# Who adds the seven products: VectorE from PSUM, or TensorE onto banks that already hold sums

## The chip, the cores and the metric

One NeuronCore of a Trainium2 chip runs the whole program in one launch. The metric is device time in microseconds (us), the median over runs. The engines have short names in what follows: PE is TensorE (matmuls), PEld its weight loads, DVE is VectorE, ACT is ScalarE, POOL is GpSimd, and SP issues DMAs. All data are fp32.

## The reference, cut to what matters

Two decoder-like layers work on `x` (2 batches x 1024 tokens x 256). Layer 0 is a windowed cross-attention and a grouped linear feed-forward, layer 1 a cross-attention with a sigmoid and then a soft mixture of experts. The change is in the last of these only:

```python
logits = jnp.einsum('bsd,etd->bset', xn, se)          # 1024 tokens x 1024 slots
dispatch = jax.nn.softmax(logits, axis=1)
slots = jnp.einsum('bsd,bset->betd', xn, dispatch)    # per batch: 1024 slots x 256
h = jax.nn.gelu(slots @ w1, approximate=False)        # w1: 256 x 1024   <- the change
processed = h @ w2                                    # w2: 1024 x 256
combine = jax.nn.softmax(logits.reshape(b, s, e * t), axis=-1)
out = jnp.einsum('bnd,bsn->bsd', processed.reshape(b, e * t, d), combine)
```

The product `slots @ w1` of each batch is 1024 x 256 by 256 x 1024.

## The kernel before, in words

**The stage.** `hidden(b)` computes gelu(slots @ w1) of batch `b`, transposed: 1024 hidden units on the partitions, in eight chunks of 128, and 1024 slots along the free dimension, in two halves of 512. It runs twice (b = 0, 1), each time between `gather` (slots from dispatched tokens, line 409, whose last transposes are `pst`, line 450) and `processed` (h @ w2, products `pp`, line 586), which `combined` follows (products `pc`, also line 586).

**Seven products instead of eight.** The 2 x 2 block product is made in the Strassen-Winograd way. `sum_weights` has made the seven left blocks `lefts` from w1, `sum_slots` makes the seven right blocks from the slots on DVE: `t1` (line 498), `t2` (line 500), a difference in place (line 501), `t4` (line 502). Chunks j and j + 4 go together, so there are four groups, j = 0 to 3, and in each the products are, by their index in `lefts` and `rights`:

- p1 (index 0) and p2 (index 1): the slots as they are. p1 and p2 of a group need none of the sums.
- p5 (index 4) uses t1, p6 (index 5) uses t2, p7 (index 6) the difference of line 501, p4 (index 3) uses t4, p3 (index 2) the slots of the other half.

With u = p1 + p6 the four results are h11 = p1 + p2, h12 = u + p5 + p3, h21 = u + p7 + p4 and h22 = u + p7 + p5. Each goes through gelu on ACT into the `mh` tiles, which `processed` reads.

**How a product is made.** In the version before, `alone(i, j)` takes a PSUM bank of its own and issues one 128x128 by 128x512 matmul into it (line 511; the trace shows each as two matmul records). PSUM has eight banks in two pools of four (`ps_0`, `ps_1`), which successive allocations take in turn. p1 is copied to SBUF by ACT (line 545, `begin`); after that DVE makes the additions of the group, each with one operand in SBUF and one in PSUM, result in SBUF (lines 552, 556, 557, 561, 563, 567 and 570): seven of them. Four gelus per group (line 521) read and write SBUF in place.

**What sets the order.** `manual_schedule(engines=IN_ORDER)` keeps PE and DVE in the order in which the code names the instructions; before, it stands around the first three products, `turn_slots` and `sum_slots` only, and the rest of `hidden` is placed by the scheduler. ACT is in program order from the logits on (`ACT_ORDER`, line 1349), so it takes its instructions as written: the last `dispatch(1, 7)` (line 398, the exponential of the last 128 tokens of batch 1, which follows a POOL addition of line 395) comes before the first copy of `hidden(0)`. `turn(1, 0, True)`, four 128x512 transposes on DVE (line 308) and sixteen DMAs, is done inside `hidden(0)`, after group 1.

Of the kernel before, what the change touches and what calls it, by code (L numbers as in the profile page):

```python
# [10 lines left out]
AF = mybir.ActivationFunctionType  # L11
ALU = mybir.AluOpType
# [22 lines left out]
OC = FF // P  # L35
# [7 lines left out]
EC = NSLOT // P  # L43
# [4 lines left out]
IN_ORDER = {mybir.EngineType.DVE, mybir.EngineType.PE}  # L48
# [4 lines left out]
def tile_kernel(  # L53
# [19 lines left out]
    nc = tc.nc  # L73
# [9 lines left out]
    def bank(name, side=0):  # L83
        return ps[side].tile([P, 512], FP, tag="bank", name=name)
# [92 lines left out]
    def in_order(x, dc):  # L177

        return x[:, :, dc].rearrange("p i t n -> p t i n")
# [110 lines left out]
    def turn(q, h, late=False, move=True):  # L290

        if q < QB:
            tr = pools["m12"].tile(
                [P, R4, EC // 2, QT, SQ], FP, tag="tr", name=f"tr_{q}_{h}", bufs=2
            )
        else:

            if h == 0:
                trs[q] = keep[0].tile(
                    [P, 2, R4, EC // 2, QT, SQ], FP, tag=f"ec_{q % QB}", name=f"tr_{q}"
                )
            tr = trs[q][:, h]
        half = ecs[q][:, h]
        for t in range(QT):
            ins = nc.vector.transpose(  # L308
                tr[:, :, :, t, :].rearrange("p r c n -> p c r n"),
                half[:, t, :].rearrange("p (c r n) -> p c r n", c=EC // 2, r=R4),  # L310
            )
            if late:
                tc.keep_in_program_order(ins)
        turned_squares[q, h] = tr
        if move:
            turn_moves(q, h)
# [3 lines left out]
    def turn_moves(q, h):  # L320
        half, tr = ecs[q][:, h], turned_squares[q, h]
        to = half.rearrange("p a b -> p (a b)").rearrange("p (k i n) -> p k i n", i=R4, n=SQ)
        for i in range(R4):
            for r in range(R4):
                nc.sync.dma_start(
                    out=to[ts(r, SQ), :, i, :],
                    in_=tr[ts(i, SQ), r].rearrange("p c t n -> p (c t) n"),
                )
# [115 lines left out]
    def turn_slots(b, c):  # L444

        if c % 2 == 0:
            pts[c // 2] = bank(f"pst_{b}_{c // 2}", 1)
        pt = pts[c // 2]
        for dc in range(DC):
            nc.tensor.transpose(  # L450
                pt[:, ds(dc * 2 * P + (c % 2) * P, P)], sls[c][:, ts(dc, P)], ident
            )
        if c == EC - 3:
            for dc in range(DC):
                slots_out(b, c // 2, dc)

    def slots_out(b, c2, dc):
        nc.vector.tensor_scalar(
            slTs[b][1][:, dc, ts(c2 - 2, 2 * P)], pts[c2][:, ts(dc, 2 * P)],
            gx[:, dc : dc + 1], None, ALU.mult,  # L460
        )
# [18 lines left out]
    def sum_slots(b):  # L480

        x, y = slTs[b]
        b11, b21 = in_order(x, 0), in_order(x, 1)
        b12, b22 = y[:, 0, :], y[:, 1, :]

        def by_square(v):
            return v.rearrange("p (t i n) -> p t i n", t=QT, i=R4)


        t0, t1_ = (  # L490
            keep[b].tile([P, QT, XW], FP, tag=f"xh_{i}", name=f"sl_sums_{b}_{i}").rearrange(
                "p t d -> p (t d)"
            )
            for i in range(2)
        )
        t1, t2, t4 = t0[:, 0:512], t0[:, 512:1024], t1_[:, 0:512]
        slots_out(b, EC // 2 - 1, 0)
        nc.vector.tensor_tensor(by_square(t1), by_square(b12), b11, ALU.subtract)
        slots_out(b, EC // 2 - 1, 1)
        nc.vector.tensor_tensor(t2, b22, t1, ALU.subtract)  # L500
        nc.vector.tensor_tensor(b12, b22, b12, ALU.subtract)
        nc.vector.tensor_tensor(by_square(t4), b21, by_square(t2), ALU.subtract)
        rights[b] = [b11, b21, b22, t4, t1, t2, b12]

    def hidden(b):


        def alone(i, j):
            to = bank(f"pmh_{b}_{j}_{i}", nb[0] % 2)
            nb[0] += 1  # L510
            nc.tensor.matmul(  # L511
                to,
                lhsT=lefts[i][:, ts(j, P)],
                rhs=in_order(slTs[b][0], i) if i < 2 else rights[b][i],
                start=True,
                stop=True,
            )
            return to

        def gelu(h):  # L520
            nc.scalar.activation(h, h, AF.Gelu)  # L521

        NU = OC // 2

        with tc.manual_schedule(engines=IN_ORDER):
            p1s = [alone(0, 0)]
            turn_slots(b, EC - 1)
            p1s.append(alone(0, 1))
            p2 = alone(1, 0)
            sum_slots(b)  # L530
        hs = {}

        def begin(j):

            for g in range(2):
                for u in range(2):
                    fc = j + u * NU
                    if fc % 2 == 0:
                        hss[b, g, fc // 2] = keep[b].tile(
                            [P, 2, 512], FP, tag=f"lg_{4 * g + fc // 2}", name=f"mh_{b}_{g}_{fc}"  # L540
                        )
            hs[j] = [
                hss[b, g, (j + u * NU) // 2][:, j % 2, :] for g in range(2) for u in range(2)
            ]
            nc.scalar.copy(hs[j][0], p1s[j])  # L545

        begin(0)
        for j in range(NU):
            h11, h21, h12, h22 = hs[j]
            p5 = alone(4, j)  # L550
            p6 = alone(5, j)
            ins = nc.vector.tensor_tensor(h12, h11, p6, ALU.add)
            if b == 0 and j == 2:
                tc.keep_in_program_order(ins)
            p7 = alone(6, j)
            nc.vector.tensor_tensor(h21, h12, p7, ALU.add)
            nc.vector.tensor_tensor(h22, h21, p5, ALU.add)  # L557
            gelu(h22)
            if j + 1 < NU:
                begin(j + 1)  # L560
            nc.vector.tensor_tensor(h12, h12, p5, ALU.add)
            p4 = alone(3, j)
            nc.vector.tensor_tensor(h21, h21, p4, ALU.add)
            gelu(h21)
            if j > 0:
                p2 = alone(1, j)
            nc.vector.tensor_tensor(h11, h11, p2, ALU.add)
            gelu(h11)
            p3 = alone(2, j)
            nc.vector.tensor_tensor(h12, h12, p3, ALU.add)  # L570
            gelu(h12)
            if j + 2 < NU:
                p1s.append(alone(0, j + 2))
            if b == 0 and j == 1:
                turn(1, 0, True)

    nb = [0]

# [220 lines left out]
    with (  # L799
# [124 lines left out]
        with tc.tile_pool(name="p0", bufs=1) as p0, tc.tile_pool(name="a0", bufs=2) as a0:  # L924
# [52 lines left out]
            for c in range(C0):  # L977
                for dc in range(DC):
# [4 lines left out]
                        start=(dc == 0),  # L983
# [6 lines left out]
            for c in range(C0):  # L990
                for dc in range(DC):
# [4 lines left out]
                        start=(dc == 0),  # L996
# [10 lines left out]
            for dc in range(DC):  # L1007
                pws = [bank(f"pwk_{dc}_{e}") for e in range(2)]
                for c in range(C0):
                    for e in range(2):  # L1010
# [5 lines left out]
                            start=True,  # L1016
# [9 lines left out]
            for g in range(NBW // 2):  # L1026
                pw = bank(f"pvw_{g}")
                for i in range(2):
                    for c in range(C0):
# [4 lines left out]
                            start=True,  # L1034
# [102 lines left out]
        with (  # L1137
# [36 lines left out]
            for c in range(C1):  # L1174
                for dc in range(DC):
# [4 lines left out]
                        start=(dc == 0),  # L1180
# [14 lines left out]
            for dc in range(DC):  # L1195
# [4 lines left out]
                    start=(dc == 0),  # L1200
# [6 lines left out]
            for b in range(B):  # L1207
                for e in range(2):
                    to = vblk1[e * NK : (e + 1) * NK, b, :, e, :]
# [63 lines left out]
            for c in range(C1):  # L1273
# [4 lines left out]
                    start=True,  # L1278
# [8 lines left out]
            for q in range(NQ):  # L1287
                b = q * QN // S
                oTs[q] = a1.tile([P, C1, QN], FP, tag="oT", name=f"oT_{q}")
                for c in range(C1):  # L1290
# [8 lines left out]
                    for j in range(NPR):  # L1299
# [5 lines left out]
                            start=True,  # L1305
# [26 lines left out]
                    for j in range(NPR):  # L1332
# [4 lines left out]
                            start=True,  # L1337
# [20 lines left out]
    for u in range(1, B * ST + 2):  # L1358
        b, s = divmod(u, ST)
# [31 lines left out]
    for b in range(B):  # L1391
# [25 lines left out]
        if b == 0:  # L1417
            dispatch(1, ST - 1)
        hidden(b)
        with tc.manual_schedule(engines=IN_ORDER):  # L1420
            processed(b)
# [70 lines left out]
```

## Time and profile before

| | |
|---|---|
| device time, median of 3 runs | 423.03 us (422.97 to 423.04) |
| span of the profiled execution, first to last instruction | 421.3 us |
| around the span (median less span) | 1.7 us |
| granted TensorE clock over the span | 0.999 |
| PE busy | 416.1 us (99%) |
| DVE busy | 316.7 us (75%) |
| ACT busy | 131.1 us (31%) |
| products of `hidden` (L511), 56 matmuls, two records each | 592 ns a record, one every 0.43 us |
| additions of `hidden` on DVE, 56 | 0.68 us each, one every 0.60 us |
| gelus of `hidden` on ACT, 32 | 0.63 us each |

The profiled execution has no time of its own outside its span; the sum is made on the span, and the 1.7 us around it are taken as fixed.

How to read it: busy time of PE says only that matmuls overlap one another; whether PE waited is seen from the starts of its records. In a timeline the first column is the start of a run of like instructions in us from the start of the span, the second its length, `xN` how many, and the bracket at the end the idle time of the engine before it and who ended it.

### The profile page before, as it was taken

The numbers are of one execution on the slowest core, as the hardware profiler recorded it, in microseconds if no ns is written. First come the engines' busy times: TensorE is split into PE (matmuls) and PEld (weight loads), VectorE is DVE, ScalarE is ACT, GpSimd is POOL, SyncE is SP. The second block draws the span as 40 slices with busy tenths as digits, with TensorE's granted clock in tenths as the row PEclk, the third lists the DMA queues.
The fourth block names the chain that finished last, engine by engine and source line by source line (L and its number), as shares of the span: only waits on it lengthen the run. The fifth ranks groups of instructions, "written<-read, shape, count | busy, mean of one in ns | idle before, by whom it ended". The sixth has DMA issues, their size and how long they took to land.

```text
span 421.3 us, 6298 instructions
## 1 busy us (share of the span) xinstructions
PE 416.1 (99%) x2270; PEld 310.4 (74%) x2270; DVE 316.7 (75%) x712; ACT 131.1 (31%) x265; POOL 73.8 (18%) x86
## 2 busy tenths in 40 slices
PE   9999999999999999999999999999999999999996
PEld 7888988888444454444488744999998864499996
DVE  2676878745578669978769889977985589776956
ACT  1145568513444522244641554300000004420000
POOL 2112333211101220104948900000000000000000
PEclk9999999999999999999999999999999999999999
DMA  6999993404523332120052664450022566620003
GB/s 255 418 414 426 376 366 122 181 36 123 149 102 103 47 49 31 29 44 2 0 213 102 125 99 73 68 88 2 0 85 48 120 122 97 91 42 2 2 2 100
DMA packets 99425, 50.03 MB, mean 119 GB/s; under 512 B 87873, under 2 KB 94401, under 8 KB 97857
## 3 DMA queue, kind: packets, MB, share of 16 engines
q1 hardware_dynamic: 99394, 49.63, 42.1%
q8 instruction: 18, 0.29, 0.3%
q14 instruction: 13, 0.11, 0.1%
HBM read 32.74 MB, written 6.30 MB: 93 GB/s over the span
## 4 chain that ended last, share of the span: by engine, by line
PE 89%; DVE 7%; issue 1%; POOL 1%; ACT 1%; DVEq 0%; ACTq 0%
PE psl L409 13%; PE pmt L879 13%; PE pc L586 12%; PE pp L586 12%; PE pmh L511 10%; PE pl L256 7%; PE pq L1233 3%; PE po L907 3%; PE pf L1247 3%; PE psg L1301 2%; PE psc L1055 2%; PE poT L1333 2%; PE po L1101 2%; DVE lg L264 1%; PE pvw L1030 1%
## 5 line engine op out<-in xcount | busy, mean ns | idle before, releaser
L879 PE MATMUL pmt<-wg 128*128 128x256 f32 x256 | 58.9, 386 | 0.1
L409 PE MATMUL psl<-xh,lg 128*128 128x258 f32 x256 | 56.8, 380 | 0.0
L256 PE MATMUL pl<-seT,xhT 128*128 128x512 f32 x128 | 56.1, 594 | 0.2 <-DVE rmax L275 0.2
L879 PEld LDWEIGHTS pmt<-wg 128*128 128x128 f32 x256 | 48.9, 193 | 7.8 <-ACT wg L868 0.5
L409 PEld LDWEIGHTS psl<-xh,lg 128*128 128x128 f32 x256 | 48.1, 190 | 7.4 <-issue 0.5
L256 PEld LDWEIGHTS pl<-seT,xhT 128*128 128x128 f32 x128 | 24.1, 190 | 29.2 <-issue 25.7
L395 POOL TENSOR_TENSOR lg<-lg,mb 128x1024 f32<-128x1024 f32 x13 | 33.2, 2591 | 27.2 <-ACT mb L203 25.3
L279 ACT ACTIVATE ec<-lg,nm 128x1024 f32<-128x1024 f32 x16 | 18.4, 1148 | 39.7 <-DVE nm L264 38.0
L586 PEld LDWEIGHTS pp<-ms,mh 128*128 128x128 f32 x256 | 29.4, 192 | 1.3 <-issue 0.7
L586 PE MATMUL pp<-ms,mh 128*128 128x128 f32 x256 | 30.0, 276 | 0.1
L521 ACT ACTIVATE mh<-mh 128x512 f32<-128x512 f32 x32 | 19.2, 628 | 20.8 <-DVE mh L557 19.2
L511 PE MATMUL pmh<-slT,ms 128*128 128x512 f32 x48 | 24.2, 592 | 0.0
L868 ACT ACTIVATE wg<-wg,less 128x255 f32<-128x255 f32 x56 | 23.3, 495 | 0.1
L1310 ACT ACTIVATE sg<-psg 128x512 f32<-128x512 f32 x32 | 16.5, 602 | 18.2 <-PE psg L1301 18.2
L586 PE MATMUL pp<-m_sums,mh 128*128 128x128 f32 x192 | 22.1, 275 | 0.0
L586 PE MATMUL pc<-pr,ec 128*128 128x128 f32 x192 | 22.1, 275 | 0.0
L586 PEld LDWEIGHTS pp<-m_sums,mh 128*128 128x128 f32 x192 | 21.8, 192 | 0.0
L586 PEld LDWEIGHTS pc<-pr,ec 128*128 128x128 f32 x192 | 21.8, 192 | 0.0
L398 ACT ACTIVATE lg<-lg 128x1024 f32<-128x1024 f32 x16 | 16.1, 1045 | 18.2 <-POOL lg L395 18.2
L545 ACT COPY mh<-pmh 128x512 f32<-128x512 f32 x8 | 4.6, 570 | 50.2 <-PE pmh L511 50.2
L308 DVE STREAM_TRANSPOSE tr<-ec 128x512 f32<-128x512 f32 x32 | 19.8, 674 | 0.0
L597 DVE TENSOR_TENSOR mh<-mh,mh 128x1024 f32<-128x1024 f32 x16 | 18.5, 1218 | 0.5 <-PE pp L586 0.5
(193 smaller groups left out, 670.6 us busy)
## 6 DMA issues: line engine op xcount, KB each, us to landing
wg<-in_wff_dram SPq DMA_DIRECT2D x5, 2052.0 KB, 10.2
ec<-tr SPq DMA_DIRECT2D x128, 64.0 KB, 2.3
wg<-in_wff_dram SPq DMA_DIRECT2D x4, 1026.0 KB, 12.7
xT<-in_xT_dram SPq DMA_DIRECT2D x4, 512.0 KB, 13.8
x<-in_x_dram SPq DMA_DIRECT2D x4, 512.0 KB, 15.9
d_a<-tr_a SPq DMA_DIRECT2D x4, 512.0 KB, 2.6
hTa<-d_a SPq DMA_DIRECT2D x16, 128.0 KB, 3.0
xhT<-tr_m SPq DMA_DIRECT2D x64, 32.0 KB, 2.0
```

What stands on the lines that cost most here:

```text
L256: nc.tensor.matmul(pl, lhsT=xhTs[q][:, dc, ts(t, P)], rhs=in_order(seT[:, n], dc), start=(dc == 0), stop=(dc == DC - 1),)
L279: nc.scalar.activation(ecs[q][:, :, t, :], lg.rearrange("p (h n) -> p h n", h=2), AF.Exp, bias=nm[:, 1:2], scale=-1.0, accum_out=zcs[b][:, ...
L308: ins = nc.vector.transpose(tr[:, :, :, t, :].rearrange("p r c n -> p c r n"), half[:, t, :].rearrange("p (c r n) -> p c r n", c=EC // 2, ...
L395: engine.tensor_tensor(lgs[b][s], lgs[b][s], mbs[b], ALU.add)
L409: nc.tensor.matmul(pz[:, 0:XW], lhsT=lgs[b][s][:, ts(c, P)], rhs=xhs[b * QB + s // QT][:, s % QT, :], start=(s == 0), stop=(s == ST - 1),)
L511: nc.tensor.matmul(to, lhsT=lefts[i][:, ts(j, P)], rhs=in_order(slTs[b][0], i) if i < 2 else rights[b][i], start=True, stop=True,)
L521: nc.scalar.activation(h, h, AF.Gelu)
L586: nc.tensor.matmul(to, lhsT=left(k, m), rhs=right[:, k, :], start=(k == 0), stop=(k == QT - 1),)
L597: nc.vector.tensor_tensor(dst, x, y, op)
L868: nc.scalar.activation(w, w, AF.Identity, bias=less[:, oc : oc + 1])
L879: nc.tensor.matmul(pm[:, ts(hc, D)], lhsT=w1g[:, oc, ts(hc, P)], rhs=w2g[:, oc, :], start=(oc == 0 and hc == 0), stop=(oc == OC - 1 and hc ...
L1310: nc.scalar.activation(sg[:, j, :], psgs[j], AF.Tanh, scale=0.5 * DH1**-0.5)
```

## The change

Per group there are now three PSUM banks, a, b and c, in place of seven:

- bank a: p1, copied to SBUF by ACT as before; then p2 is accumulated onto it by PE, and gelu reads the bank (h11).
- bank b: p6, to which DVE adds the copy of p1 in place; later p7 is accumulated onto it by PE, DVE adds p5 to that into SBUF (h22, then gelu in place), and last p4 is accumulated onto it, and gelu reads the bank (h21).
- bank c: p5, copied to SBUF by ACT (a copy that was not there before); DVE writes bank b + that copy into bank c; p3 is accumulated onto it, and gelu reads the bank (h12).

So DVE makes three additions a group, two of which write PSUM, ACT two copies and four gelus, three of which read PSUM, and PE seven matmuls, four of them onto a bank that holds something. All of `hidden` is now in written order on PE and DVE. The written order is also another one: p2 of group 0 comes before p6 and p5 as it did, but p6 now stands before p5, groups 0 and 1 start together, and p7 and p3 of a group come one group later, p4 two groups later. In the built program the first two `pp` matmuls of `hidden(0)`'s successor stand before its last five products.

```diff
-        def alone(i, j):
-            to = bank(f"pmh_{b}_{j}_{i}", nb[0] % 2)
-            nb[0] += 1
+        def onto(key, i, j, first=True):
+            if first:
+                banks[key, j] = bank(f"pmh_{b}_{j}_{key}", nb[0] % 2)
+                nb[0] += 1
+            to = banks[key, j]
             nc.tensor.matmul(
                 to,
                 lhsT=lefts[i][:, ts(j, P)],
                 rhs=in_order(slTs[b][0], i) if i < 2 else rights[b][i],
-                start=True,
+                start=first,
                 stop=True,
+                skip_group_check=not first,
             )
...
-        with tc.manual_schedule(engines=IN_ORDER):
-            p1s = [alone(0, 0)]
-            turn_slots(b, EC - 1)
-            p1s.append(alone(0, 1))
-            p2 = alone(1, 0)
-            sum_slots(b)
...
-        begin(0)
-        for j in range(NU):
-            h11, h21, h12, h22 = hs[j]
-            p5 = alone(4, j)
-            p6 = alone(5, j)
-            ins = nc.vector.tensor_tensor(h12, h11, p6, ALU.add)
...
-            p7 = alone(6, j)
-            nc.vector.tensor_tensor(h21, h12, p7, ALU.add)
-            nc.vector.tensor_tensor(h22, h21, p5, ALU.add)
-            gelu(h22)
-            if j + 1 < NU:
-                begin(j + 1)
-            nc.vector.tensor_tensor(h12, h12, p5, ALU.add)
-            p4 = alone(3, j)
-            nc.vector.tensor_tensor(h21, h21, p4, ALU.add)
-            gelu(h21)
-            if j > 0:
-                p2 = alone(1, j)
-            nc.vector.tensor_tensor(h11, h11, p2, ALU.add)
-            gelu(h11)
-            p3 = alone(2, j)
-            nc.vector.tensor_tensor(h12, h12, p3, ALU.add)
-            gelu(h12)
-            if j + 2 < NU:
-                p1s.append(alone(0, j + 2))
-            if b == 0 and j == 1:
-                turn(1, 0, True)
+        def p1(j):
+            begin(j)
+            nc.scalar.copy(hs[j][0], onto("a", 0, j))
+        def p2(j):
+            onto("a", 1, j, first=False)
+        def gelu_11(j):
+            gelu(hs[j][0], banks["a", j])
+        def p6(j):
+            t = onto("b", 5, j)
+            nc.vector.tensor_tensor(t, t, hs[j][0], ALU.add)
+        def p5(j):
+            t = onto("c", 4, j)
+            nc.scalar.copy(hs[j][3], t)
+            nc.vector.tensor_tensor(t, banks["b", j], hs[j][3], ALU.add)
+        def p7(j):
+            t = onto("b", 6, j, first=False)
+            nc.vector.tensor_tensor(hs[j][3], t, hs[j][3], ALU.add)
+            gelu(hs[j][3], hs[j][3])
+        def p3(j):
+            gelu(hs[j][2], onto("c", 2, j, first=False))
+        def p4(j):
+            gelu(hs[j][1], onto("b", 3, j, first=False))
+        with tc.manual_schedule(engines=IN_ORDER):
+            p1(0)
+            turn_slots(b, EC - 1)
+            p1(1)
+            p2(0)
+            sum_slots(b)
+            p6(0)
+            p5(0)
+            p6(1)
+            p5(1)
+            gelu_11(0)
+            p2(1)
+            gelu_11(1)
+            p7(0)
+            p3(0)
+            for j in range(2, NU):
+                p1(j)
+                p4(j - 2)
+                p6(j)
+                p5(j)
+                if j > 2:
+                    p2(j - 1)
+                    gelu_11(j - 1)
+                p7(j - 1)
+                p3(j - 1)
+                if b == 0 and j == 2:
+                    turn(1, 0)
+            p7(NU - 1)
+            p4(NU - 2)
+            p3(NU - 1)
+            p2(NU - 1)
+            gelu_11(NU - 1)
+            p4(NU - 1)
```

More of the change, by code (lines that the diff above doesn't have):

```diff
@@ L505, in hidden @@
     def hidden(b):
-        def alone(i, j):
-            to = bank(f"pmh_{b}_{j}_{i}", nb[0] % 2)
-            nb[0] += 1
+        NU = OC // 2
+        banks = {}
+        def onto(key, i, j, first=True):
[3 more added lines that the diff above has]
+            to = banks[key, j]
             nc.tensor.matmul(
@@ L514, in alone, with gelu @@
                 rhs=in_order(slTs[b][0], i) if i < 2 else rights[b][i],
-                start=True,
+                start=first,
                 stop=True,
+                skip_group_check=not first,
             )
             return to
-        def gelu(h):
-            nc.scalar.activation(h, h, AF.Gelu)
-        NU = OC // 2
-        with tc.manual_schedule(engines=IN_ORDER):
-            p1s = [alone(0, 0)]
-            turn_slots(b, EC - 1)
-            p1s.append(alone(0, 1))
-            p2 = alone(1, 0)
-            sum_slots(b)
+        def gelu(dst, src):
+            nc.scalar.activation(dst, src, AF.Gelu)
         hs = {}
@@ L544, in begin @@
             ]
-            nc.scalar.copy(hs[j][0], p1s[j])
-        begin(0)
-        for j in range(NU):
-            h11, h21, h12, h22 = hs[j]
-            p5 = alone(4, j)
-            p6 = alone(5, j)
-            ins = nc.vector.tensor_tensor(h12, h11, p6, ALU.add)
-            if b == 0 and j == 2:
-                tc.keep_in_program_order(ins)
-            p7 = alone(6, j)
-            nc.vector.tensor_tensor(h21, h12, p7, ALU.add)
-            nc.vector.tensor_tensor(h22, h21, p5, ALU.add)
-            gelu(h22)
-            if j + 1 < NU:
-                begin(j + 1)
-            nc.vector.tensor_tensor(h12, h12, p5, ALU.add)
-            p4 = alone(3, j)
-            nc.vector.tensor_tensor(h21, h21, p4, ALU.add)
-            gelu(h21)
-            if j > 0:
-                p2 = alone(1, j)
-            nc.vector.tensor_tensor(h11, h11, p2, ALU.add)
-            gelu(h11)
-            p3 = alone(2, j)
-            nc.vector.tensor_tensor(h12, h12, p3, ALU.add)
-            gelu(h12)
-            if j + 2 < NU:
-                p1s.append(alone(0, j + 2))
-            if b == 0 and j == 1:
-                turn(1, 0, True)
+        def p1(j):
+            begin(j)
+            nc.scalar.copy(hs[j][0], onto("a", 0, j))
```

## The prediction

> **What bounds the kernel now.** First the page: busy times, and the engines' shares of the chain that ended last.
>
> ```profile
> PE 416.1 (99%) x2270; PEld 310.4 (74%) x2270; DVE 316.7 (75%) x712; ACT 131.1 (31%) x265; POOL 73.8 (18%) x86
> PE 89%; DVE 7%; issue 1%; POOL 1%; ACT 1%; DVEq 0%; ACTq 0%
> ```
>
> PE carries the chain; DVE has 7% of it. The question is whether that DVE share lies in the changed stage, so next come the windows: the two passes of `hidden`, from p1 of group 0 to the first `pp` (columns: stretch, its length, then busy time of PE, PEld, DVE, ACT and POOL, granted clock, DMA share, GB/s).
>
> ```profile
> 239.20:264.30 25.10, 24.73 (x60) 10.69 (x59) 22.97 (x38) 13.62 (x21) 2.65 (x2) 1.00 0.59 88
> 343.30:367.80 24.50, 24.50 (x61) 10.75 (x59) 20.59 (x35) 9.85 (x17) 0.00 (x0) 1.00 0.63 94
> ```
>
> DVE is busy 92% and 84% of them, but PE is the one that never stops: 28 products of two records each, at one record per 0.43 us (the timeline's pairs start 0.86 apart), are 28 x 0.858 = 24.02 us, and two `pst` records at 0.11 lie among them: 24.24. From the first p1 to the first `pp` they take 25.10 (239.25 to 264.35) and 24.43 (343.37 to 367.80). So DVE, busy as it is, holds PE up by about 1 us in the two together, and the timeline shows that it does so at the front. First batch 0, then batch 1:
>
> ```profile
> 239.25 1.02 PE L511 MATMUL pmh<-slT,ms 128*128 128x512 f32 x2
> ...
> 240.33 1.88 PE L511 MATMUL pmh<-slT,ms 128*128 128x512 f32 x4
> ...
> 241.89 1.06 ACT L398 ACTIVATE lg<-lg 128x1024 f32<-128x1024 f32 x1 [0.80 <-POOL lg L395]
> ...
> 242.55 2.22 PE L511 MATMUL pmh<-sl_sums,m_sums 128*128 128x512 f32 x4 [0.34 <-DVE sl_sums L498]
> 242.83 0.69 DVE L500 TENSOR_TENSOR sl_sums<-slT,sl_sums 128x512 f32<-128x512 f32 x1
> 242.85 0.57 ACT L545 COPY mh<-pmh 128x512 f32<-128x512 f32 x1
> ```
>
> ```profile
> 344.88 1.45 PE L511 MATMUL pmh<-slT,ms 128*128 128x512 f32 x3
> ...
> 346.17 2.06 PE L511 MATMUL pmh<-sl_sums,m_sums 128*128 128x512 f32 x4
> 346.29 0.69 DVE L500 TENSOR_TENSOR sl_sums<-slT,sl_sums 128x512 f32<-128x512 f32 x1
> ```
>
> In batch 0 p1 of groups 0 and 1 and p2 run from 239.25, 240.33 and 241.19 (third record of the x4). Then p5 and p6 wait for t1 and t2: p5 starts 0.15 after L498 ended at 242.40, p6's bank follows t2 (L500, ends 243.52). p2 holds PE until 242.05, so 0.50 is idle before p5. Four records without a wait last 1.88 (the line of 240.33); these four last 2.22, which is 0.34 more. The front of batch 0 idles 0.84, that of batch 1, where p5 follows at once and the four last 2.06, 0.18. Note the copy of p1 (L545): it starts only at 242.85, because ACT is in order and has L398 ahead of it, which waited for POOL. Now nobody on PE needs that copy.
>
> At the other end, from the critical chain in order of time:
>
> ```profile
> 264.96 1.24 ACT mh L521 x2
> 266.19 0.04 issue
> 266.24 23.71 PE pp L586 x210
> ```
>
> The first `pp` products wait for the last gelus. Their 64 records should take 64 x 0.1117 = 7.15 us and take 7.57 in batch 0 and 7.24 in batch 1: 0.42 and 0.09 idle. After that no PE start is late by over 0.04 us until the last matmul. All idle time of PE that the stage has is therefore 0.84 + 0.42 + 0.18 + 0.09 = 1.53 us.
>
> **What the change removes.** Of 56 DVE additions 32 go, at 0.60 us a start: 19.2 us of DVE. All of that lies beside PE work, since PE starts a record each 0.43 us without a break between the two ends; it is worth nothing there. Per group of 6.01 us on PE (7 x 0.858), DVE falls from 4.2 to 1.8 us, ACT rises from 3.0 to 3.5 (one more copy, 0.53 from start to start). Both stay below PE, with the four transposes of L308 (2.4 us) and the one ACT table load (1.28 us) included. Seven matmuls remain seven. That four of them add onto a bank costs nothing by the trace: L256 does this with its second `dc` step, and its records mean 594 ns to L511's 592.
>
> **What it adds on PE's path: the front of batch 0.** p2 now accumulates onto the bank that ACT copies p1 from, so it waits for L545, and p6 and everything after it are queued behind p2 on PE, which is in order. L545 ends at 242.85 + 0.57 = 243.42; its start can't move, since L398 and POOL ahead of it are untouched. From the end of a releasing instruction to the matmul it is 0.15 after DVE (242.40 to 242.55) and 0.05 after ACT (the chain's 266.19 to 266.24); I take 0.13, since this start also has to load weights, and keep 0.05 to 0.25. p2 starts at 243.55. PE is free from 241.19, so it idles 2.36, and 0.08 more as after each stop (0.504 in place of 0.429 to the next record). t2 is ready at 243.52 by then, so p6 follows without a wait, and the old 0.84 is gone: 2.44 - 0.84 = +1.60.
>
> **The front of batch 1.** ACT is idle there and copies p1 at 344.43 to 345.02, before p2's turn at 345.31: no wait. But p6 now comes before p5, and p6 needs t2. L500 ends at 346.29 + 0.69 = 346.98, p6 starts 0.15 later at 347.13, where p5 used to start at 346.17 on t1. Idle 0.96 + 0.08 less the old 0.18: +0.86. In batch 0 the same exchange is hidden by the longer wait.
>
> **The middle.** Followed through the written order with the durations above, every other wait is met before PE gets there. The tightest is p4 of group 1: it needs p7's addition, which DVE makes after the addition of group 2 into bank c, and that has 0.3 us to spare. What no row shows is a DVE addition that writes PSUM. Rows around it: 0.68 with PSUM read and SBUF written (L556), 0.69 all in SBUF (L500), 0.75 for the slowest undisturbed 128x512 row on a PSUM input (L264), 1.36 for L498 when it ran beside POOL. I take 0.68, as it is the same instruction with one operand moved. It could also be 0.60, which gives nothing back. At 1.0 for all three additions the stage loses 0.8 more in the two batches, at 1.36 it loses 5.3.
>
> **The end.** p4 of group 3 is now the last product, and one gelu stands between it and `pp`. Its result is complete 1.02 after its first record starts (0.43 + 0.59), gelu takes 0.04 + 0.63, the next start 0.13: 1.82. PE has 0.86 of its own and, in batch 0, four k-steps of `pp` at 0.22: 1.75, so 0.07 idle. In batch 1 six k-steps cover it. The old 0.42 and 0.09 shrink to 0.07 and 0: -0.35 and -0.09. DVE frees up earlier for `processed`, but its next addition (L597) waits for the `pp` products themselves, so nothing is gained behind.
>
> **Sum.** Batch 0: 1.60 - 0.35 = +1.25. Batch 1: 0.86 - 0.09 = +0.77. Together +2.0 us on the span of 421.3, that is 423.3; with the 1.7 around it 425.0 against the median of 423.03 (+0.48%). A difference under 0.2% (0.85 us) can't be told from none.
>
> **The clock.** A pause of PE can cost more than itself. The last matmul starts at 417.80 and ends at 418.08, and the windows show the clock thereafter:
>
> ```profile
> 418.00:419.00 1.00, 0.08 (x1) 0.00 (x0) 0.35 (x1) 0.00 (x0) 0.00 (x0) 1.00 0.83 267
> 419.00:420.00 1.00, 0.00 (x0) 0.00 (x0) 0.00 (x0) 0.00 (x0) 0.00 (x0) 1.00 0.64 208
> 420.00:421.30 1.30, 0.00 (x0) 0.00 (x0) 0.00 (x0) 0.00 (x0) 0.00 (x0) 0.54 0.00 0
> ```
>
> A mean of 0.54 over the last 1.3 us puts the step to half at about 420.1, 2.0 us after the last matmul ended. The new pause in batch 0 is 2.2 us, counted likewise from 241.35 (end of p1 of group 1) to 243.55. What half pace looks like is at the start: L879 has 6 records in 4.80 to 6.90 and 12 in 8.20 to 10.30, the first matmul having begun at 1.04. [...] The row would let the clock halve, and rival 1 prices that from rows alone; one step at the end of a program doesn't settle it.
>
> **Rivals.**
> 1. *The clock drops in batch 0's pause.* For it: the step 2.0 us after the last matmul. Against: matmuls ran before and after, and no other pause in this trace is over 0.5 us, so none shows it. Half pace ends somewhere up to 7 us later (8.2 less 1.0 at the start), which loses 0 to 3.5; with the middle of that, 1.75, it gives 426.8.
> 2. *A DVE write into PSUM is dear.* At 1.0 us each 425.8, at 1.36 430.3. Against: four forms of DVE operand here all take 0.67 to 0.75.
> 3. *Faster: the copy isn't the last to come.* If ACT took L545 before L398, p2 would start at its old 241.19, and with t2 ahead of PE too the four idle times could all close: at most -1.53, or 421.5; with the ends alone, 422.5. It decides at a copy that is over by 241.1 in batch 0; in the profile it is over at 243.42 and behind an instruction that POOL releases at 241.85.
> 4. *No change:* the front's loss is made good because PE's pause lets something later run without a wait. Against it: there is no later idle time of PE to make it good from except the 0.5 that is already in the sum. 423.0 to 423.8.
>
> **How the numbers follow.** The forecast, with small shifts of its waits (0.05 to 0.25 after ACT moves the total from 1.8 to 2.2), 0.66; rival 1 0.17; rival 2 0.08; rival 3 0.04; rival 4 0.05. Slower by over 0.2%: 0.66 + 0.17 + 0.08 = 0.91. The likeliest case alone lies in 424.6 to 425.4; the range is taken from 424.3 to 427.0, so that it holds the cheaper half of rivals 1 and 2; about 0.10 is left out above and 0.09 below.
>
> **What would show it right or wrong.** Right: in batch 0 p2 starts near 243.55, released by ACT's L545, and in batch 1 p6 near 347.1 plus the first batch's 1.25, released by L500; the rest of the 28 products at 0.43 a record; DVE's busy time some 19 us lower; PE busy time about the same with a span 2.0 longer. Wrong: p2 of batch 0 starting at 241.2, records of 0.86 after the pause (the clock), or PE waiting for DVE in the middle of a group.

## The result: 0.6% slower, and where the time went

| | before | after |
|---|---|---|
| device time, median | 423.00 us (422.70 to 423.04, 4 runs) | 425.66 us (424.65 to 426.75, 4 runs) |
| ratio after to before | | 1.0064, 95% interval 1.0043 to 1.0085 |
| profiled execution: time, span | span 421.3 us | 424.86 us, span 423.0 us |
| batch 0, first `pmh` record to first `pc` record | 50.54 us | 51.66 us |
| batch 1, the same | 49.53 us | 50.24 us |
| `combined` of batch 0 to `hidden` of batch 1 | 53.58 us | 53.58 us |

The four runs of the changed kernel are two pairs: 424.65 and 424.86 us at a granted clock of 1.000, 426.46 and 426.75 at 0.996, and the median lies between the pairs. The profile is of the lower pair. Its two stages are 1.12 + 0.71 = 1.83 us longer than before, and `hidden` began 0.10 earlier in it: together the 1.7 us by which the spans differ. The upper pair costs another 1.85 us, to which `longer` and the paragraph on rival 1 come back.

The page of the changed kernel, the lines that answer to those of before (busy times; then the engines' shares of the chain that ended last):

```profile
PE 414.6 (98%) x2270; PEld 309.2 (73%) x2270; DVE 297.8 (70%) x680; ACT 134.4 (32%) x273; POOL 73.7 (17%) x86
PE 77%; POOL 8%; DVE 6%; issue 3%; SPq 2%; DMA 2%; ACT 1%; POOLq 1%; DVEq 0%; ACTq 0%
```

DVE has 32 instructions and 18.9 us less, PE has as much to do as it had, and the span is longer. POOL, 1% of the chain before, now has 8%: the chain no longer runs along PE into `hidden` but arrives by POOL's additions and the exponential behind them. Both stages by window (length, then busy time of PE, PEld, DVE, ACT, POOL):

```profile
239.10:265.45 26.35, 24.29 (x63) 10.97 (x62) 16.56 (x26) 15.95 (x26) 2.60 (x2) 1.00 0.54 81
344.30:369.60 25.30, 24.59 (x61) 10.76 (x60) 14.65 (x23) 12.69 (x23) 0.00 (x0) 1.00 0.65 98
```

PE is now idle for 2.06 us of the first and 0.71 of the second, though DVE is busy only 63% and 58% of them. The timeline puts each idle stretch in one place. Batch 0:

```profile
240.23 1.02 PE L515 MATMUL pmh_a<-slT,ms 128*128 128x512 f32 x2
241.73 1.06 ACT L398 ACTIVATE lg<-lg 128x1024 f32<-128x1024 f32 x1 [0.79 <-POOL lg L395]
242.68 0.69 DVE L500 TENSOR_TENSOR sl_sums<-slT,sl_sums 128x512 f32<-128x512 f32 x1
242.69 1.05 ACT L545 COPY mh<-pmh_a 128x512 f32<-128x512 f32 x2
243.31 1.12 PE L515 MATMUL pmh_a<-slT,ms 128*128 128x512 f32 x2 [2.06 <-ACT mh L545]
244.28 1.02 PE L515 MATMUL pmh_b<-sl_sums,m_sums 128*128 128x512 f32 x2
```

ACT's exponential waits 0.79 us for POOL, the copy of p1 comes behind it, and p2 waits 2.06 us for that copy. By then t2 (242.68 + 0.69 = 243.37) is ready and p6 follows p2 without a wait. Batch 1:

```profile
345.47 1.88 PE L515 MATMUL pmh_a<-slT,ms 128*128 128x512 f32 x4
347.31 0.69 DVE L500 TENSOR_TENSOR sl_sums<-slT,sl_sums 128x512 f32<-128x512 f32 x1
348.05 1.13 PE L515 MATMUL pmh_b<-sl_sums,m_sums 128*128 128x512 f32 x2 [0.71 <-DVE sl_sums L500]
```

p2 goes straight on behind p1 of group 1 (the x4), and p6, which now precedes p5, waits 0.71 us for t2. Between these two fronts and `pp` no record is late. The end of batch 0, from the critical chain:

```profile
264.63 0.86 PE pmh_a L515 x2
265.49 0.86 PE pmh_b L515 x2
266.34 5.75 PE pp L616 x51
```

PE reaches `pp` without a stop; before, two gelus of ACT and a chain of DVE additions stood there.

### The profile page after: what moved, and what is told of

Same layout as the page of the kernel before. It is cut to its first block, busy times and chain, and to the rows that moved or that the text cites. A ratio compares the mean times of both kernels' runs of the same rounds, so it can differ in the third digit from the quotient of the medians.

```text
span 423.0 us, 6257 instructions
## 1 busy us (share of the span) xinstructions
PE 414.6 (98%) x2270; PEld 309.2 (73%) x2270; DVE 297.8 (70%) x680; ACT 134.4 (32%) x273; POOL 73.7 (17%) x86
## 4 chain that ended last, share of the span: by engine, by line
PE 77%; POOL 8%; DVE 6%; issue 3%; SPq 2%; DMA 2%; ACT 1%; POOLq 1%; DVEq 0%; ACTq 0%
PE pmt L909 12%; PE pp L616 12%; PE pc L616 12%; PE psl L409 7%; POOL lg L395 6%; PE pl L256 5%; PE pmh_b L515 5%; PE pq L1263 3%; PE po L937 3%; PE pmh_c L515 3%; PE pmh_a L515 2%; SPq L158 2%; PE psc L1085 2%; PE pf L1277 2%; PE po L1131 2%
## 5 line engine op out<-in xcount | busy, mean ns | idle before, releaser
L909 PE MATMUL pmt<-wg 128*128 128x256 f32 x256 | 57.8, 380 | 1.0 <-DVE wg L900 0.9
L909 PEld LDWEIGHTS pmt<-wg 128*128 128x128 f32 x256 | 47.8, 189 | 8.8 <-DVE wg L900 1.9
L545 ACT COPY mh<-pmh_a 128x512 f32<-128x512 f32 x8 | 4.6, 582 | 50.7 <-PE pmh_a L515 50.7
L616 PE MATMUL pc<-pr_sums,ec 128*128 128x128 f32 x160 | 18.5, 275 | 0.0
L515 PE MATMUL pmh_a<-slT,ms 128*128 128x512 f32 x32 | 16.3, 596 | 2.1 <-ACT mh L545 2.1
```

Source lines behind the costliest of these rows:

```text
L515: nc.tensor.matmul(to, lhsT=lefts[i][:, ts(j, P)], rhs=in_order(slTs[b][0], i) if i < 2 else rights[b][i], start=first, stop=True, skip_gr ...
L616: nc.tensor.matmul(to, lhsT=left(k, m), rhs=right[:, k, :], start=(k == 0), stop=(k == QT - 1),)
L909: nc.tensor.matmul(pm[:, ts(hc, D)], lhsT=w1g[:, oc, ts(hc, P)], rhs=w2g[:, oc, :], start=(oc == 0 and hc == 0), stop=(oc == OC - 1 and hc ...
```

## The experiments

Theory: the two fronts are all that the change costs. p2 of batch 0 waits for an ACT copy that is queued behind an exponential, and p6 of batch 1 waits for t2, having been put ahead of p5; the 32 additions less are worth nothing while PE is late there. Rivals: the PSUM writes of DVE or PE's accumulation cost something; the clock drops in the pause and accounts for the rest; and, against the prediction's own words, DVE's load did bound something in the kernel before. Medians are over all runs of a kernel, each with its own runs of the kernel before on the same chip: 423.04 us (22 runs) for the first four, 422.97 (18) for the next four, 423.00 (15) for the last two. The ratio is estimated from all the single runs and can differ from that of the two medians by some 0.001.

| kernel | median us (lowest to highest, runs) | ratio to before, 95% interval | stage of batch 0, batch 1, us |
|---|---|---|---|
| `p5_first` | 424.26 (423.93 to 425.77, 9) | 1.0033, 1.0023 to 1.0043 | 51.67, 49.44 |
| `copy_first` | 424.23 (424.06 to 425.04, 8) | 1.0026, 1.0015 to 1.0037 | 51.01, 50.23 |
| `both` | 422.62 (422.49 to 423.32, 11) | 0.9990, 0.9981 to 0.9999 | 50.36, 49.45 |
| `filled` | 424.99 (424.70 to 425.72, 5) | 1.0046, 1.0033 to 1.0058 | 51.87, 50.24 |
| `longer` | 427.46 (425.86 to 427.74, 5) | 1.0099, 1.0086 to 1.0111 | 54.24, 50.24 |
| `after_again` | 424.90 (424.64 to 426.33, 6) | 1.0054, 1.0041 to 1.0067 | 51.67, 50.24 |
| `ahead` | 421.65 (421.45 to 421.76, 6) | 0.9967, 0.9956 to 0.9979 | 49.38, 49.27 |
| `before_ahead` | 423.15 (422.95 to 423.38, 11) | 1.0004, 0.9996 to 1.0013 | 50.80, 49.36 |
| `ahead_2` | 421.98 (421.82 to 422.11, 9) | 0.9976, 0.9966 to 0.9985 | 49.52, 49.51 |
| `turn_later` | 421.83 (421.58 to 421.99, 7) | 0.9971, 0.9959 to 0.9982 | 49.35, 49.50 |

**`p5_first`: one front alone.** The changed kernel, with p5 of group 0 ahead of p6 on PE, as it was before.

```diff
             sum_slots(b)
+            p5_copy(0)     # product p5 into bank c, copied by ACT
             p6(0)
-            p5(0)
+            p5_add(0)      # DVE: bank b + that copy into bank c
             p6(1)
```

> One edit against the changed kernel: in group 0 p5 comes before p6 on PE and its copy before p6's addition (the addition into bank c stays after that of bank b). The theory of the front (each waits for what its first product needs): batch 1 loses its pause before p6, so its front is 0.9 us shorter; batch 0, where the copy of p1 is the last to come, is unchanged. 423.9 us in executions where the clock holds, 1.8 more where it drops in batch 0's pause, which is as long as before. Rival (the additions that write PSUM or the accumulating matmuls cost the time, spread over the groups): 424.7 or 426.6, no change.

Batch 1 falls from 50.24 to 49.44 us and batch 0 stays. The front of batch 1 in its timeline:

```profile
345.46 1.88 PE L515 MATMUL pmh_a<-slT,ms 128*128 128x512 f32 x4
347.18 1.02 PE L515 MATMUL pmh_c<-sl_sums,m_sums 128*128 128x512 f32 x2
348.14 1.96 PE L515 MATMUL pmh_b<-sl_sums,m_sums 128*128 128x512 f32 x4
```

p5 follows on t1 without a pause, and p6 starts where it did in the changed kernel, behind work instead of behind a gap. The exchange of p5 and p6 costs 0.80 us by the stage, and 0.86 by the two profiled executions (424.86 to 424.00).

**`copy_first`: the other front alone.** The exponential goes behind the copies of p1 on ACT.

```diff
             p1(1)
+            if b == 0:
+                dispatch(1, ST - 1)
             p2(0)
...
-        if b == 0:
-            dispatch(1, ST - 1)
         hidden(b)
```

> One edit against the changed kernel: in batch 0 the last exponential (L398) comes after the two copies of p1 on ACT. Theory of the front: the copy of p1 is over near 241.4, p2 starts near 241.5 and p6 near 243.5 (t2), so of the pause of 2.2 us some 0.4 and 1.1 remain: 424.1 us. Neither part is long enough for the clock to drop, so there is one group of times and no second one 1.8 higher. Rival on the clock (the second group of times has another cause than the pause): two groups, 424.1 and 425.9. Rival on the middle of the groups: 424.7.

```profile
241.75 1.05 ACT L545 COPY mh<-pmh_a 128x512 f32<-128x512 f32 x2
242.37 1.13 PE L515 MATMUL pmh_a<-slT,ms 128*128 128x512 f32 x2 [0.23 <-ACT mh L545]
242.69 1.06 ACT L398 ACTIVATE lg<-lg 128x1024 f32<-128x1024 f32 x1
244.43 1.10 PE L515 MATMUL pmh_b<-sl_sums,m_sums 128*128 128x512 f32 x2 [0.94 <-DVE sl_sums L500]
```

The copy now comes as soon as PE has made p1, and the 2.06 us of p2 fall to 0.23. But p6 stops next, 0.94 us, for t2, which the longer wait had hidden: of some 1.8 us gained at one instruction 0.65 arrive in the stage. This profiled execution took 425.04 us and entered the stage 0.88 us later than the changed kernel's, before anything that is edited; the other seven runs took 424.06 to 424.43. Single runs of `p5_first` (424.74, 425.04), `both` (423.32) and `filled` (425.72) also lie 0.7 to 1.0 us above the others of their kernel at a clock of 1.000; they weren't profiled, and what delayed them isn't shown.

**`both`.** The two edits together.

> The edits of the two runs before together: p5 ahead of p6 in group 0, and the last exponential after the copies of p1. Theory of the front: batch 0 idles 0.4 before p2 and 0.3 before p6 (t2), batch 1 0.2 in all: 422.3 to 422.5 us, 0.5 below the kernel before, since the ends are short as well; one group of times. If accumulating on PE or writing PSUM cost anything in the middle, it stays above 423.

```profile
241.04 1.05 ACT L545 COPY mh<-pmh_a 128x512 f32<-128x512 f32 x2
241.65 1.12 PE L515 MATMUL pmh_a<-slT,ms 128*128 128x512 f32 x2 [0.46 <-ACT mh L545]
242.61 1.07 PE L515 MATMUL pmh_c<-sl_sums,m_sums 128*128 128x512 f32 x2
243.71 1.95 PE L515 MATMUL pmh_b<-sl_sums,m_sums 128*128 128x512 f32 x4
```

The two edits together take 2.1 us off the full-clock time of the changed kernel (424.76, the median of its six such runs) and bring it 0.1% under the kernel before. The order of exponential and copy was the same in the kernel before, where no matmul waited for the copy. What is left is a wait that belongs to accumulation itself: p2 needs the copy of p1 out of the bank, 0.46 us here.

**`filled`: does the pause cost more than its length?** The changed kernel, with eight 128x128 matmuls into a spare bank in batch 0's pause; their result isn't used.

```diff
             p1(1)
+            if b == 0:
+                spare = bank("spare", 1)
+                for _ in range(8):
+                    nc.tensor.matmul(spare[:, 0:P], lhsT=ones, rhs=ones, start=True, stop=True)
             p2(0)
```

> The changed kernel with eight 128x128 matmuls of ones into a spare bank on PE in batch 0's pause, after p1 of group 1 (8 x 0.22 = 1.8 us, less than the 2.2 of the pause); their result isn't used. [...]

PE's idle stretch shrinks to 0.49 us, the stage is no shorter for it (51.87 us), and no run of the five is at 0.996. Alone that is too few runs to say that none would be.

**`longer`: a longer pause.** The changed kernel with one more exponential on ACT ahead of the copy; its result isn't used.

```diff
             dispatch(1, ST - 1)
+            again = keep[0].tile([P, NSLOT], FP, tag="lg_7", name="again")
+            nc.scalar.activation(again, lgs[1][ST - 1], AF.Exp, scale=-1.0)
         hidden(b)
```

> The changed kernel with one more 128x1024 exponential on ACT (its result isn't used) between the last L398 and the copy of p1 in batch 0: the pause of PE grows by one start-to-start time of such an exponential, 0.95 us, to 3.2 us. Theory of the front: 425.7 us where the clock holds. [...] Rival (the wait for the copy is hidden or the clock has no part): all near 425.7 or 424.7.

Four of five runs are at 0.995 or 0.996 and take 427.26 to 427.74 us, the fifth, at 0.999, 425.86. The profile is of one of the four. Its wait and the two products behind it, then the windows around them (the last three columns: granted clock, DMA share, GB/s):

```profile
244.52 2.08 PE L515 MATMUL pmh_a<-slT,ms 128*128 128x512 f32 x2 [3.04 <-ACT mh L545]
246.39 1.72 PE L515 MATMUL pmh_b<-sl_sums,m_sums 128*128 128x512 f32 x2
247.95 0.59 PE L515 MATMUL pmh_c<-sl_sums,m_sums 128*128 128x512 f32 x1
```

```profile
244.00:244.38 0.38, 0.00 (x0) 0.00 (x0) 0.38 (x2) 0.38 (x2) 0.00 (x0) 1.00 0.45 65
244.40:247.78 3.38, 3.26 (x4) 1.52 (x5) 0.29 (x1) 0.56 (x2) 0.00 (x0) 0.50 0.65 98
247.80:249.00 1.20, 1.20 (x4) 0.57 (x3) 0.70 (x1) 0.00 (x0) 0.00 (x0) 1.00 0.68 101
```

The clock is at half from 244.4 to 247.8: 3.4 us, in which four records are done at 0.86 us. Then it is full again. Half a clock for 3.4 us is 1.7 us lost, and the four runs lie 1.4 to 1.9 above the fifth.

**`after_again`.** The changed kernel once more, on the chip of `longer`.

> The changed kernel once more, for the share of executions in the upper group of times. Theory of the clock: times of about 424.7 and about 426.6 with nothing between, the upper ones at a mean granted clock lower by 0.004, in about three to five of ten. Rival (two chips or two launches, not two executions): all times of this job in one group.

Two groups again: 424.64 to 424.93 at full clock (4 runs), 426.29 and 426.33 at 0.996.

**`ahead`: no front left.** p1 of groups 2 and 3 is issued ahead of everything that waits, p5 ahead of p6 in groups 0 and 1, p2 of group 0 behind both. Here gelu of h11 of groups 2 and 3 overwrites the copy of p1 before the addition of p6 reads it, so values differ while instructions, shapes and their number stay.

```diff
             p1(1)
-            p2(0)
+            p1(2)
+            p1(3)
             sum_slots(b)
+            p5_copy(0)
             p6(0)
-            p5(0)
+            p5_add(0)
+            p2(0)
...
             p3(0)
+            p2(2)
+            gelu_11(2)
             for j in range(2, NU):
-                p1(j)
+                if j == 3:
+                    p2(3)
+                    gelu_11(3)
...
```

> The changed kernel in another written order: p1 of groups 2 and 3 right after p1 of group 1, then p5, p6 and p2 of group 0, p5, p6 and p2 of group 1; p2 of groups 2 and 3 earlier too; the same products, copies, additions and gelus. Theory of the front: PE has work until t1, t2 and the copy are there, so it idles neither in batch 0 nor in batch 1 (the last waits stay at 0.1): 421.4 us, 1.6 below the kernel before, in one group of times. If the middle costs anything (PSUM writes, bank releases), it stays above 422.

```profile
239.20:264.50 25.30, 25.30 (x69) 11.71 (x68) 17.03 (x27) 16.87 (x29) 2.67 (x2) 1.00 0.55 82
342.10:367.00 24.90, 24.90 (x67) 11.36 (x65) 14.62 (x23) 13.16 (x24) 0.00 (x0) 1.00 0.66 98
```

PE never stops in either window, and the time is 1.3 us under the kernel before, 0.25 above the 421.4 that was expected. Rival "PSUM writes or accumulation are dear" falls here: the products lie at 0.43 us a record with all of them in place.

**`before_ahead`: the same cure for the kernel before.** If the gain of `ahead` is the front's alone, p1 of group 2 issued ahead should bring the kernel before, with its seven additions, as far.

```diff
             p1s.append(alone(0, 1))
+            p1s.append(alone(0, 2))
             p2 = alone(1, 0)
...
-            if j + 2 < NU:
+            if 2 < j + 2 < NU:
                 p1s.append(alone(0, j + 2))
```

> The kernel before with one edit: p1 of group 2 is issued right after p1 of group 1, ahead of p2 of group 0; the seven additions on DVE stay. It tells the order from the additions. Theory (only the order at the front counts, DVE has slack in the middle): the front's idle 0.84 and 0.18 go, the waits at the end (0.42 and 0.09) stay: 422.0 us. Rival (DVE bounds the groups once the front is closed): 422.6 to 423.0.

It doesn't: 423.15 us, no change. PE at the end of batch 0's stage, and DVE in the same time:

```profile
262.73 1.02 PE L511 MATMUL pmh<-slT,m_sums 128*128 128x512 f32 x2
263.59 1.50 PE L587 MATMUL pp<-ms,mh 128*128 128x128 f32 x12
265.83 2.43 PE L587 MATMUL pp<-ms,mh 128*128 128x128 f32 x16 [0.74 <-ACT mh L521]
```

```profile
262.51 0.69 DVE L557 TENSOR_TENSOR mh<-mh,pmh 128x512 f32<-128x512 f32 x1 [0.46 <-DVE mh L553]
263.23 0.69 DVE L558 TENSOR_TENSOR mh<-mh,pmh 128x512 f32<-128x512 f32 x1
263.84 0.68 DVE L562 TENSOR_TENSOR mh<-mh,pmh 128x512 f32<-128x512 f32 x1
264.44 0.68 DVE L564 TENSOR_TENSOR mh<-mh,pmh 128x512 f32<-128x512 f32 x1
```

PE reaches `pp` 0.76 us earlier than before (263.59 to 264.35) and stops there instead: 0.9 and 0.27 us for two gelus, which wait for additions that DVE makes one after the other until well behind the last product. With the late records after these stops PE loses 1.38 us there, against 0.42 in the kernel before: the front's gain of batch 0 is given back at the far end (stage 50.80 us, before 50.54), and only batch 1 is shorter (49.36, before 49.53). That points at DVE as the bound of batch 0's stage right behind the front; the next run tests it.

**`turn_later`: that DVE is the bound, by itself.** `before_ahead`, with the four transposes of `turn(1, 0)` moved from the middle of `hidden(0)` to the start of `processed`. All 56 additions stay; the sixteen DMAs of the transposes move with them.

```diff
-            if b == 0 and j == 1:
-                turn(1, 0, True)
...
             sum_rights(right, t1, t2, t4, True)
+            turn(1, 0)
             turn(1, 1)
```

> The kernel before with p1 of group 2 issued ahead, as in before_ahead, and besides the four transposes of turn(1, 0) on VectorE (2.4 us, with their DMAs) moved from the middle of the first hidden stage to the front of the first processed stage. Theory (once the front is closed VectorE bounds the stage of batch 0 in the kernel before, so that the additions that the change removes are worth something there): the wait ahead of the pp products of batch 0, 1.4 us in before_ahead, falls to 0.1 to 0.4 us and the time from 423.15 to 421.9 to 422.3 us. Rival (the wait is that of the last addition and gelu behind the last product, whatever VectorE had to do before): the wait stays at 1.2 to 1.4 us and the time at 423.0 to 423.3 us. Rival (the transposes come too late where they go): the wait at the front of hidden's second run or in the gather ahead of it grows, 423.4 us or more.

```profile
257.74 6.01 PE pmh L511 x14
263.75 10.36 PE pp L585 x92
```

```profile
262.73 1.02 PE L511 MATMUL pmh<-slT,m_sums 128*128 128x512 f32 x2
264.33 0.68 DVE L571 TENSOR_TENSOR mh<-mh,pmh 128x512 f32<-128x512 f32 x1
```

The chain goes through `hidden` into `pp` on PE alone, the stage of batch 0 is 49.35 us, and the time 421.83 us: 1.3 us less than `before_ahead` for 2.4 us of DVE work out of the way. The last product starts at 262.73 in both runs, but the last addition (L571) at 264.33, in `before_ahead` at 265.63, and PE loses 0.09 us at `pp`. An addition takes 0.68 to 0.69 us in both, so the DMAs that moved along hadn't slowed DVE. That settles it for DVE's load, and against "the wait is that of the last addition and gelu behind the last product, whatever DVE had to do before": the same seven additions of the last group, in the same order, end 1.3 us sooner and cost almost nothing. Batch 1 gives back 0.14 us (49.50 against 49.36).

**`ahead_2`: the changed kernel with its fronts mended, computing the reference.** The exponential behind the copies, p1 of group 2 ahead, p5 before p6.

```diff
             p1(1)
+            if b == 0:
+                dispatch(1, ST - 1)
+            p1(2)
             p2(0)
             sum_slots(b)
+            p5_copy(0)
             p6(0)
-            p5(0)
+            p5_add(0)
...
-                if j > 2:
-                    p2(j - 1)
-                    gelu_11(j - 1)
                 p7(j - 1)
                 p3(j - 1)
+                if j == 2:
+                    p2(2)
+                    gelu_11(2)
```

> The changed kernel with three moves: in batch 0 the last exponential of batch 1 stands on ScalarE behind the copies of p1, p1 of group 2 is issued ahead of p2 of group 0, and p5 of group 0 stands before p6; p2 of group 2 goes to the end of its iteration. It computes the reference. Theory (the pauses at the two fronts are all that the change costs, and with them closed the additions that are gone from VectorE are worth something at the far end): p2 of group 0 waits for nothing, PE makes its 28 products at 0.86 us in both batches without a pause over 0.1 us, stage of batch 0 49.4 us, of batch 1 49.3 us, against 50.5 and 49.5 in the kernel before; time 421.4 to 421.7 us, 1.3 to 1.6 us under the kernel before, and no execution at a granted clock below 0.999. Rival (it needs more than one product ahead to cover t1 and t2): 0.4 us idle remain in batch 0, time 422.0 to 422.4 us. Rival (the earlier copy only moves the wait to the last exponential and so to what follows in combine): 422.6 us or more.

421.98 us, 0.24% under the kernel before but above its 421.4 to 421.7: each batch keeps a wait of 0.19 us, and neither lies at the front.

```profile
248.16 0.69 DVE L569 TENSOR_TENSOR mh<-pmh_b,mh 128x512 f32<-128x512 f32 x1 [0.40 <-PE pmh_b L515]
248.91 1.12 PE L515 MATMUL pmh_b<-sl_sums,ms 128*128 128x512 f32 x2
```

With p1 of group 2 moved ahead, one product (p3) is left between p7 and p4 of group 0, too little to cover the addition of line 569, which must read the bank before p4 accumulates onto it.

## Why the prediction was right, and where it was wrong

**The forecast held.** It was 425.0 us; the runs of the changed kernel at full clock took 424.64 to 424.93, and the median of the first four, 425.66, is in the range of 424.3 to 427.0. That the median lies so high is chance: two of these four are at 0.996, in `after_again` two of six, and its median is 424.90. The terms, from the two profiles:

| term | predicted us | measured us |
|---|---|---|
| front of batch 0 | +1.60 | 2.22 + 0.10 - 0.84 = +1.48 |
| end of batch 0 | -0.35 | 0.06 - 0.42 = -0.36 |
| front of batch 1 | +0.86 | 0.87 + 0.10 - 0.18 = +0.79 |
| end of batch 1 | -0.09 | 0 - 0.09 = -0.09 |
| middle | 0 | 0 |
| sum | +2.0 | +1.8 |

(The first two numbers of a front: how late p2 or p6 starts against the pace of 0.43 us, and how late the next record is. The first number of an end: how late the `pp` records are in sum against their pace of 0.11 us.) The difference of 0.2 is in the fronts, and mostly in one term: from the end of the releasing instruction to the matmul 0.13 (ACT) and 0.15 (DVE) were taken, and it was 0.05 in both (L545 ended at 243.26, p2 started at 243.31; L500 ended at 348.00, p6 started at 348.05). For ACT that is the lower bound that was kept, weight load and all. For DVE 0.05 isn't the rule: in batch 0 of `copy_first` L500 ended at 244.28 and p6 started at 244.43, the 0.15 of the kernel before; why the two differ isn't shown. The rest is batch 0's exponential, which came 0.06 us sooner against PE than before. p2's and p6's releasers, L545 and L500, are those that were named.

**DVE writing PSUM** was taken at 0.68 us between 0.60 and 1.36. Line and operation, tile, shape and count, busy time, mean ns, then idle time of DVE before:

```profile
L560 DVE TENSOR_TENSOR pmh_c<-pmh_b,mh 128x512 f32<-128x512 f32 x4 | 2.8, 700 | 2.5 <-ACT mh L559 2.5
L555 DVE TENSOR_TENSOR pmh_b<-pmh_b,mh 128x512 f32<-128x512 f32 x4 | 2.8, 697 | 3.7 <-PE pmh_b L515 3.6
```

0.70 us, and rival 2 didn't come about.

**The step that failed: "it is worth nothing there".** The 19.2 us of additions were costed at nothing because PE never waited between the ends. That was true of the kernel as changed, and the sum came out right. But the reason given, PE starts a record each 0.43 us and DVE lies beside it, mistook a bound that was hidden behind another for none. The profile before had it in the critical chain of batch 0, of which the prediction read only the end:

```profile
257.64 0.87 PE pmh L511 x2
258.52 0.02 issue
258.54 0.69 DVE mh L567
...
264.24 0.69 DVE mh L563
264.93 0.02 issue
264.96 1.24 ACT mh L521 x2
```

From 258.54 to 264.93 the chain runs over DVE's additions, while PE has products to make; in batch 1 it runs over PE alone. The pause at the front gave DVE time to keep up with PE. `before_ahead` shows it: closing the front gained nothing (423.15 against 422.97). `turn_later` shows how much stood behind it: 1.3 us. The 0.42 at the end of batch 0, which the prediction put down to the last addition and gelus, was DVE's backlog; in batch 1, which has no transposes, it was 0.09, and those two numbers side by side pointed at it. The change's own gain is this one, and without its two new waits it appears: in `ahead`, 421.65 against the 423.15 of `before_ahead`.

**Rival 3's floor held.** "At most -1.53, or 421.5" for all idle time of the stage closed: `ahead` came to 421.65, `turn_later` to 421.83 and `ahead_2` to 421.98. Its condition was incomplete: with ACT taking the copy ahead of the exponential alone (`copy_first`), p2's wait fell to 0.23 us and p6's, 0.94, took its place.

**Rival 1, the clock: right in mechanism and size, in a share of the executions.** It was priced at 1.75 us on top, 426.8; the changed kernel's runs at 0.996 took 426.29 to 426.75. Of 19 executions with the pause of about 2.1 us (the changed kernel twice and `p5_first`) five are at 0.996, of five of `longer` four; of the 41 executions without it (`copy_first`, `both`, `filled`, `ahead`, `before_ahead`) none is, nor of the 16 of `ahead_2` and `turn_later`. So the clock does drop with this pause, not each time; a mean of 0.996 is what 3.4 us at half clock, the stretch in `longer`, make of 425 us. That it halves right there is seen in `longer` alone: no profile of a 2.1 us pause at 0.996 was taken. The length of a pause alone doesn't decide it: the trace before has half clock from 420.11, 2.03 us after its last matmul ended (418.08), while in the profile of the changed kernel the clock stayed full after the pause of 2.06 us, and again from the end of its last matmul (419.8) to the end of the span (423.0), 3.2 us. What decides isn't shown.

That a pause of this length costs only itself, as the forecast took it, no run shows as a rule: 14 of the 19 executions kept the clock and 5 didn't. The row at the end of the trace before was right about what can happen, and the range was held by keeping it.

## What to carry to other kernels

One bound can hide behind another: before an engine's work is costed at nothing, ask what would be late if the wait ahead of it were gone, follow the critical chain through the whole stage, and look for the same stage with less of that work (here batch 1, without the transposes). To let TensorE accumulate onto a bank that another engine must read first puts that engine's queue on TensorE's path (a wait of 2.06 us in batch 0 here), so issue products that wait for nothing between the two, and put what the reader has queued ahead of it behind. Of the two cheapest cures here one needed no new dataflow: one product issued earlier and four transposes moved gave the kernel before 421.83 us, as much as the mended change.

## What the runs showed of the hardware

- The TensorE clock dropped in 5 of 19 executions with a pause of about 2.1 us, in 4 of 5 with one of 3.0 us, and in none of 57 with a shorter one or none. In `longer` it stayed at half for 3.4 us; its four executions with the drop took 1.4 to 1.9 us longer than the fifth.
- After the last matmul the clock went to half 2.03 us later in the kernel before; in the changed kernel it was still full 3.2 us after the last matmul, at the end of the span.
- A DVE addition of 128x512 with its result in PSUM takes 0.70 us, against 0.68 with its result in SBUF.
- From the end of the ACT copy to the start of the matmul that it releases it was 0.05 us, with the weights loaded in the same moment; after a DVE subtraction 0.05 us in batch 1 and 0.15 in batch 0 of `copy_first`. After these stops the second record of a matmul started 0.07 to 0.11 us late.
